# Layer 0 of a four-layer network: work moved between ScalarE and VectorE, the first keys broadcast in two parts, and a finer order at the layer's end

## The chip, the cores and the metric

The kernel runs on one core of a Trainium2 chip. Its time is that of the device, in microseconds (us), from start to end of one execution; of several runs the median is given. The core has a matrix engine (TensorE, PE in the profile; its weight loads are PEld), a vector engine (VectorE, DVE), an engine for functions of one argument (ScalarE, ACT), a general one (GpSimd, POOL) and a queue engine for transfers (SyncE, SP). Each runs its own instructions in order and waits on semaphores for the others. Matrix products go to PSUM[...]; the rest lies in SBUF.

## The reference, cut to what matters

Four layers follow one another; the change concerns layer 0, a deformable attention with a multilayer perceptron behind it. For 2 images of 512 channels and 32 x 32 pixels, in 8 groups of 64 channels:

```python
xn = _bn(x, bn1_g, bn1_b)
q = _gconv1x1(xn, qw)
off = conv(q, off_dw_w, stride 4, 6 x 6 taps, each channel alone)
off = gelu(off + off_dw_b)
off = tanh(einsum(off, off_pw_w)) * 4.0
vgrid = 2.0 * (key's own place + off) / 7 - 1.0
kv = _grid_sample(xn, vgrid)            # bilinear, 64 keys a group
k, v = _gconv1x1(kv, kw), _gconv1x1(kv, vw)
pos = grid_q[:, :, None, :] - grid_kv[:, None, :, :]
bias = sign(pos) * log1p(abs(pos))
bias = relu(bias @ cpb_w1 + cpb_b1)
bias = relu(bias @ cpb_w2 + cpb_b2)
bias = bias @ cpb_w3 + cpb_b3
attn = softmax(q k / 8 + bias)
x = x + out_w (attn v) + out_b
x = x + mlp(_bn(x))
```

The bias costs most: for each of 16 pairs of image and group, 1024 queries times 64 keys go through two layers of 128 hidden units. All of it is in fp32.

## The kernel before, in words

**Tiles and loops.** Two groups lie on the 128 partitions at a time; the eight such pairs of groups are what the code calls pairs. A bias unit `u` is one group of one image (16 of them), and it has 8 octets `o` of 8 keys, each cut into two halves `jj` (the kernel's index for keys 0 to 31 and 32 to 63). One step of the main loop, a quad, is one (u, o, jj): four keys for all 1024 queries. There are 256 quads. For each, `first_hidden` (L475 on) lets VectorE make four tiles `h` of 128 x 1024 as a sum of a table along x and one along y (L484); `second_hidden` (L495 on) multiplies them by the second layer's weights, 64 matmuls in four column groups (L515), into four accumulators `hp`, which ScalarE evicts (L520). ScalarE and GpSimd then flip signs and GpSimd adds them up, partly with accumulating DMAs (L507). `last_product` (L547) multiplies by ones at the ends.

**Tables.** `table` (L430 on) gives each pair of octets its logs: a DMA broadcasts 16 keys' logs from DRAM to all partitions, GpSimd makes the x table (L440), and VectorE the y table for each octet (L472). The y table lies in a PSUM bank called `bank`, which also holds the taps of the convolution, the results of small products, and the x weights `wp` of the sampling. The first 16 keys of all don't go through DRAM: 32 matmuls (L449) with a column of the identity spread the logs of pair 0 to all partitions, and ScalarE evicts them (L457, L461).

**Work that goes along.** `offsets` (L279 on) and `sampled` (L361 on) are generators: the first makes a pair's queries, the convolution of 36 taps (L311: six products; L325: three reductions), Gelu, tanh, the key positions and their logs; the second the bilinear weights `w` (L377 to L397), the sampled values (L404), keys and values. Pair 0's `offsets` runs alone ahead of the main loop. The others advance by one step per quad, behind the matmuls of that quad; `attend` has the first right to such a step. `odd` holds a generator back until a quad with `jj` = 1, whose successor needs no new y table in `bank`.

**The order.** Inside layer 0, PE, ScalarE, VectorE and GpSimd run in the order in which the code is written (`manual_schedule`); a planner places what lies outside of it, such as the MLP's sums on VectorE (L672 to L675), between those instructions. PSUM has three buffers of two banks for everything in the pool `ps_h` (`hp`, the transposes, `q`), one bank for `bank`, and one for the similarities `sim`. Two engines that touch one bank of one tile are put in order with a wait.

**The end.** The last unit's attention (`attend`, L555 on) runs alone: its softmax goes back and forth between PE, VectorE and ScalarE. `share` (L193 on) lays the output projection's matmuls (L200) between those steps, for three of four output tiles; the fourth follows in `project_one` (L647), and the MLP begins.

Of the kernel before, what the change touches and what calls it, by code (L numbers as in the profile page):

```python
# [11 lines left out]
F32 = mybir.dt.float32  # L12
# [6 lines left out]
P = 128  # L19
# [23 lines left out]

G_KEY, G_QRY, G_X, G_Y = 0, 2, 2 + W, 2 + W + 1
NGRID = G_Y + NB
# [7 lines left out]
class Net:  # L53
# [43 lines left out]
    def layer0(self):  # L97
# [3 lines left out]
        with ExitStack() as ctx:  # L101
# [7 lines left out]
            self.last_weights(keep)  # L109
# [25 lines left out]
            with self.tc.manual_schedule(engines=engines):  # L135
                pairs = [{} for _ in range(BP)]
                for n, _ in enumerate(self.offsets(pairs[0], 0, ps)):
                    if n == 7:
                        nc.vector.tensor_copy(self.ys, self.grid[:, G_Y : G_Y + NB])
                        self.fold_weights()  # L140
# [42 lines left out]
                next(share)  # L183
                self.last_product(*held[1], sims, ps_s)
                for n, _ in enumerate(self.attend(u, pairs[u // 2], sims.pop(u), att, None)):
                    if n in (0, 1):
                        next(share)
                for _ in share:
                    pass
                for h in range(2):  # L190
                    self.project_one(ps, att, ow, "out_b", B - 1, CT - 1, h)

    def share(self, accs, att, w):  # L193


        nc = self.nc
        for t in range(CT):
            for o, acc in enumerate(accs):
                for h in range(2):
                    nc.tensor.matmul(  # L200
                        acc[:, h, :],
                        lhsT=w[:, t, o * P : (o + 1) * P],
                        rhs=att[t][:, h * HF : (h + 1) * HF],
                        start=(t == 0),
                        stop=(t == CT - 1),
                    )
                if t == CT - 1:
                    xt = self.xs[B - 1][o].rearrange("p (h x) -> p h x", h=2)
                    nc.vector.scalar_tensor_tensor(xt, acc, self.col("out_b", o), xt, ALU.add, ALU.add)
            if t < CT - 1:  # L210
                yield

    def last_weights(self, keep):

        nc = self.nc
        self.w3row = keep.tile([P, P], F32, tag="row", name="w3row")
        nc.scalar.dma_start(self.w3row, self.io["cpb_w3"].partition_broadcast(P))  # L220
        w3 = self.colr("w3r", 4)
        self.magb = keep.tile([P, 4], F32, tag="magb", name="magb")
        nc.vector.scalar_tensor_tensor(self.magb, w3, -1.0, w3, ALU.mult, ALU.max)
        nc.vector.tensor_tensor(self.magb, self.magb, self.colr("b2r", 4), ALU.mult)
        sign = keep.tile([P, 4], F32, tag="sign", name="sign")
        nc.vector.tensor_scalar(sign, w3, 0.0, 2.0, ALU.is_ge, ALU.mult)
        nc.vector.tensor_scalar(sign, sign, -1.0, None, ALU.add)
        self.flip = keep.tile([P, 3], F32, tag="flip", name="flip")
        nc.vector.tensor_tensor(self.flip, sign[:, 0:3], sign[:, 3:4].to_broadcast([P, 3]), ALU.mult)
        self.ends = keep.tile([P, 60], F32, tag="ends", name="ends")  # L230
        nc.vector.memset(self.ends, 0.0)
        for k in range(4):
            rows = slice(32 * k, 32 * k + 32)
            nc.vector.tensor_copy(self.ends[rows, 28 + k : 29 + k], sign[rows, 3:4])
# [44 lines left out]
    def offsets(self, m, bt, ps):  # L279
# [11 lines left out]
        q = ps.tile([P, 2, HF], F32, tag="ps", name=f"q{b}{t}")  # L291
        for par in range(2):
            rows = slice(par * DH, (par + 1) * DH)
            for h in range(2):
                nc.tensor.matmul(
                    q[h * DH : (h + 1) * DH, par, :],
# [5 lines left out]
        for par in range(2):  # L302
            for h in range(2):
                (nc.scalar.copy if h == par else nc.vector.tensor_copy)(
                    qp[par * DH : (par + 1) * DH, 1 + 16 * h : 17 + 16 * h, 1 : 1 + W],
                    q[h * DH : (h + 1) * DH, par, :].rearrange("p (r w) -> p r w", w=W),
# [3 lines left out]
        for ky in range(6):  # L310
# [13 lines left out]
        for third in (slice(0, 24), slice(24, 44), slice(44, NJ)):  # L324
            nc.vector.tensor_reduce(conv[:, third], prod[:, :, :, third].rearrange("p a b j -> p j (a b)"), AX.X, ALU.add)  # L325
            yield
        ge = self.fpool.tile([P, NJ], F32, tag="ge", name=f"ge{b}{t}")
# [8 lines left out]
        nc.scalar.activation(at, o, AF.Tanh)  # L336
        yield
# [19 lines left out]
        nc.sync.dma_start(spots, at)  # L357
# [3 lines left out]
    def sampled(self, m, bt, ps):  # L361
# [6 lines left out]
        g = self.fone.tile([P, 2, 2 * NJ], F32, tag="g", name=f"g{b}{t}")  # L368
# [4 lines left out]
        for n in range(NB):  # L373
# [3 lines left out]
        nc.vector.tensor_scalar(g, spots.rearrange("p k d -> p d k"), 1.0, W / 2.0, ALU.add, ALU.mult)  # L377
        wx = self.fone.tile([P, 2 * NJ], F32, tag="wx", name=f"wx{b}{t}")
        nc.vector.tensor_scalar(wx, g[:, 0, :], -0.5, self.grid[:, G_X : G_X + 1], ALU.add, ALU.subtract)
        nc.vector.tensor_scalar(g[:, 1, :], g[:, 1, :], -0.5, None, ALU.add)  # L380
# [3 lines left out]
            g[:, 1, :].unsqueeze(1).to_broadcast([P, NB, 2 * NJ]),  # L384
# [4 lines left out]
        nc.scalar.activation(wx, wx, AF.Abs)  # L389
        nc.scalar.activation(w, w, AF.Abs)  # L390
        yield
        nc.vector.tensor_scalar(w, w, -1.0, 1.0, ALU.mult, ALU.add)
        yield
        wp = self.bank[:, 384:512]
        nc.vector.tensor_scalar(wx, wx, -1.0, 1.0, ALU.mult, ALU.add)
        nc.vector.tensor_scalar(wp, wx, 0.0, None, ALU.max)
        nc.vector.scalar_tensor_tensor(w, w, 0.0, wp.unsqueeze(1).to_broadcast([P, NB, 2 * NJ]), ALU.max, ALU.mult)  # L397
# [32 lines left out]
    def table(self, u, o, pairs, tables):  # L430
# [12 lines left out]
        if u == o == 0:  # L443

            logs = self.ps_h.tile([P, 2, 8, 2, W], F32, tag="ps", name="lb_ps")
            for j in range(2):
                for k in range(8):
                    key = j * 32 + k
                    nc.tensor.matmul(  # L449
                        logs[:, j, k, :, :].rearrange("p d x -> p (d x)"),  # L450
                        lhsT=self.ident[:, key : key + 1].to_broadcast([P, P]),
                        rhs=pairs[0]["log"].rearrange("p d x -> p (d x)"),
                        start=True,
                        stop=True,
                    )
            x = self.tab.tile([P, 2, 8, W], F32, tag="x", name="tx00")
            nc.scalar.activation(  # L457
                x, logs[:, :, :, 0, :], AF.Identity, scale=self.col("cpb_w1", 0), bias=self.col("cpb_b1")
            )
            got = self.lpool.tile([P, 2, 8, 2, W], F32, tag="logs", name="lb00")  # L460
            nc.scalar.copy(got, logs)  # L461
            tables["logs"], tables["x"], tables["rest"] = logs, x, got
        elif o % 2 == 0:
# [4 lines left out]
        if u == 0 and o == 1:  # L468
            tables["logs"] = tables.pop("rest")
        y = self.bank[:, 0:256].rearrange("p (j i x) -> p j i x", j=2, i=4)  # L470
        i = 4 * (o % 2)
# [169 lines left out]
    def project_one(self, ps, att, w, bias: str, b: int, o: int, h: int):  # L641
# [3 lines left out]
        acc = ps.tile([P, HF], F32, tag="ps", name=f"{bias}_{b}{o}{h}")  # L645
# [993 lines left out]
def _grid():  # L1639
# [6 lines left out]
    rows[:, G_X] = p % W  # L1646
    for n in range(NB):
        rows[:, G_Y + n] = n * (P // W) + p // W
    return rows
# [73 lines left out]
```

## Time and profile before

| | |
|---|---|
| median of 3 runs | 3410.36 us (3410.17 to 3419.77) |
| profiled execution | 3411.19 us, of it 3409.2 us span |
| PE busy | 3354.4 us, 98% |
| VectorE, ScalarE, GpSimd busy | 2417.5, 2026.5, 2172.1 us |
| first matmul of the main loop (L515) | 35.62 us after the start |
| last matmul of layer 0 ends, MLP begins | 2069.91 and 2070.80 us after the start |
| L515, hidden products | 16384 matmuls (an fp32 product counts twice) |
| L484, first hidden layer | 1024 on VectorE, 1.215 us each |
| L520, evictions | 1024 on ScalarE, 1.112 us each |

The span is the time between the first and the last instruction of one execution. Busy time counts overlapping instructions once; an instruction's place is given by its line (L515 is line 515 of the kernel). Matmuls are pipelined: four that work in different column groups run at the same time, so whether PE is at its pace is read from the distance between their starts.

### The profile page before, as it was taken

To read this page: it belongs to the slowest core of one execution; us is meant where nothing else is said; L and a number is where in the kernel's file an instruction comes from. 1 tells how busy PE (TensorE), PEld (TensorE's weight loads), DVE (VectorE), ACT (ScalarE), POOL (GpSimd) and SP (SyncE) were. 2 spreads that over 40 slices of the span, in tenths; PEclk is the share of its full clock that TensorE was granted. 3 is DMA by queue.
4 is the path that set the end of the run, shared out by engine and by line. 5 is a ranking of instruction groups with operands and counts; after the bars stand their busy time and mean duration, and the time that the engine had idled before them with its cause. 6 is when DMAs were issued, how large, how long until landed. Compare 5 with 4: busy or idle time off the path is not lost.

```text
span 3409.2 us, 60195 instructions
## 1 busy us (share of the span) xinstructions
PE 3354.4 (98%) x25248; PEld 1246.9 (37%) x25248; DVE 2417.5 (71%) x2591; ACT 2026.5 (59%) x2109; POOL 2172.1 (64%) x1642
## 2 busy tenths in 40 slices
PE   6999999999999999999999999999999999999999
PEld 2333333333333333333333334444555433355433
DVE  6876877777776676777776665565465689765897
ACT  5787877877877687877877771111121466213662
POOL 3777878877877577877878874333333448444474
PEclk9999999999999999999999999999999999999999
DMA  5878877877877577877878862111000100000001
GB/s 150 158 150 157 160 147 153 164 147 150 167 145 147 118 152 155 164 148 149 167 157 167 160 134 107 37 50 37 0 1 0 38 1 1 14 0 13 1 1 51
DMA packets 102382, 342.63 MB, mean 101 GB/s; under 512 B 12624, under 2 KB 14288, under 8 KB 99024
## 3 DMA queue, kind: packets, MB, share of 16 engines
q0 software_dynamic: 73296, 266.90, 41.2%
q1 hardware_dynamic: 27792, 69.68, 7.1%
q8 instruction: 202, 3.31, 0.4%
q10 hardware_dynamic: 1008, 2.06, 0.2%
q14 instruction: 84, 0.69, 0.1%
HBM read 67.27 MB, written 4.46 MB: 21 GB/s over the span
## 4 chain that ended last, share of the span: by engine, by line
PE 90%; DVE 6%; POOL 2%; ACT 1%; DMA 1%; issue 1%; DVEq 0%; ACTq 0%; POOLq 0%; SPq 0%
PE hp L515 50%; PE s L1323 5%; PE o L1352 5%; PE sim L547 3%; PE qk20P L1109 1%; PE qk30P L1109 1%; PE m_0P L686 1%; PE m_6P L686 1%; PE m_3P L686 1%; PE m_2P L686 1%; PE m_1P L686 1%; PE qk31P L1109 1%; PE qk21P L1109 1%; PE m_5P L686 1%; PE m_4P L686 1%; PE m_7P L686 1%
## 5 line engine op out<-in xcount | busy, mean ns | idle before, releaser
L515 PE MATMUL hp<-h,w 128*32 128x512 f32 x16384 | 1822.4, 593 | 5.3 <-DVE h L484 3.6
L484 DVE CUSTOM_DVE_ANT_1 h<-tx,bank 128x1024 f32<-128x1024 f32 x1024 | 1180.0, 1215 | 277.1 <-PE hp L515 241.6
L520 ACT ACTIVATE h<-hp,magb 128x1024 f32<-128x1024 f32 x1024 | 1121.8, 1112 | 405.1 <-PE hp L515 398.4
L515 PEld LDWEIGHTS hp<-h,w 128*32 128x32 f32 x16384 | 530.5, 110 | 1221.7 <-issue 1154.6
L507 POOL DMA_DIRECT2D h<-h x509 | 451.8, 1021 | 411.3 <-ACT h L526 350.5
L533 POOL TENSOR_TENSOR h<-h,h 128x1024 f32<-128x1024 f32 x255 | 610.3, 2393 | 21.3
L531 POOL TENSOR_SCALAR h<-h,flip 128x1024 f32<-128x1024 f32 x256 | 446.6, 1745 | 0.9 <-ACT h L520 0.9
L1327 ACT ACTIVATE e<-s 128x1024 f32<-128x1024 f32 x256 | 261.9, 1025 | 159.6 <-PE s L1323 158.3
L522 ACT ACTIVATE h<-h,flip 128x1024 f32<-128x1024 f32 x256 | 291.4, 1138 | 0.0
L1352 PE MATMUL o<-e,v 64*64 64x512 f32 x2048 | 267.7, 589 | 0.8 <-ACT e L1327 0.8
L1323 PE MATMUL s<-q,k 64*64 64x512 f32 x2048 | 267.9, 589 | 0.0
L1332 POOL TENSOR_TENSOR some<-e,e 128x1024 f32<-128x1024 f32 x32 | 75.6, 2364 | 171.7 <-DVE sum L1341 138.7
L1334 POOL TENSOR_TENSOR some<-some,e 128x1024 f32<-128x1024 f32 x64 | 166.8, 2607 | 24.9 <-ACT e L1327 21.2
L524 POOL TENSOR_SCALAR h<-h,flip 128x1024 f32<-128x1024 f32 x128 | 144.5, 1129 | 47.7 <-ACT h L520 46.6
L526 ACT ACTIVATE h<-h,flip 128x1024 f32<-128x1024 f32 x128 | 145.6, 1138 | 0.0
L547 PE MATMUL sim<-h,ends 128*32 128x512 f32 x1024 | 142.4, 592 | 0.0
L1352 PEld LDWEIGHTS o<-e,v 64*64 64x64 f32 x2048 | 83.4, 133 | 137.4 <-issue 132.2
L1323 PEld LDWEIGHTS s<-q,k 64*64 64x64 f32 x2048 | 83.2, 133 | 136.0 <-issue 123.7
L664 POOL TENSOR_TENSOR mlp_w<-mlp_w 128x512 f32<-128x512 f32 x16 | 22.4, 1402 | 160.8 <-DMA mlp_w<-in_mlp_w 136.3
L1337 DVE TENSOR_TENSOR sum<-e,e 128x1024 f32<-128x1024 f32 x32 | 79.5, 2484 | 64.0 <-ACT e L1327 63.9
L745 ACT ACTIVATE mh<-mh,cols 128x512 f32<-128x512 f32 x64 | 46.1, 722 | 124.3 <-DVE mh L763 65.5
L1375 DVE RECIPROCAL r<-r 128x512 f32<-128x512 f32 x32 | 107.3, 3353 | 1.1
(530 smaller groups left out, 3343.9 us busy)
## 6 DMA issues: line engine op xcount, KB each, us to landing
h<-h POOLq DMA_DIRECT2D x509, 512.0 KB, 6.5
lb<-logs SPq DMA_DIRECT2D x63, 512.0 KB, 5.2
mlp_w<-in_mlp_w SPq DMA_DIRECT2D x16, 1024.0 KB, 4.9
x<-in_x SPq DMA_DIRECT2D x8, 512.0 KB, 9.5
qkw<-in_l_qk SPq DMA_DIRECT2D x2, 2048.0 KB, 8.1
out<-x SPq DMA_DIRECT2D x16, 256.0 KB, 2.7
vw<-in_l_v SPq DMA_DIRECT2D x2, 1024.0 KB, 7.9
projw<-in_l_proj SPq DMA_DIRECT2D x2, 1024.0 KB, 4.8
```

The lines of the kernel that those rows point to most:

```text
L484: self.nc.vector._custom_dve(TENSOR_ADD_SAT, out=h[:, k, :, :], in0=x[:, jj, 2 * r + k, :].unsqueeze(1).to_broadcast([P, H, W]), in1=y[:, ...
L507: nc.gpsimd.dma_start(to, what, accum_op=ALU.add)
L515: nc.tensor.matmul(hp[rows, cut], lhsT=self.l0w2[:, 32 * q : 32 * q + 32], rhs=h1[k][:, cut], start=True, stop=True)
L520: nc.scalar.activation(y, hp, AF.Relu, bias=self.magb[:, q : q + 1])
L522: nc.scalar.activation(ys[0], ys[0], AF.Copy, scale=self.flip[:, 0:1])
L531: nc.gpsimd.tensor_scalar(y, y, self.flip[:, 2:3], 1.0, ALU.mult, ALU.mult)
L533: (nc.vector if final else nc.gpsimd).tensor_tensor(y, y, ys[2], ALU.add)
L547: nc.tensor.matmul(sims[u][at : at + 32, :], lhsT=self.ends[:, 28 - 4 * o : 60 - 4 * o], rhs=z[jj][:, h * HF : (h + 1) * HF], start=(o == ...
L686: self.nc.tensor.matmul(acc[p], lhsT=w[:, a, k, p * P : (p + 1) * P], rhs=right(r, k), start=k == 0, stop=k == 1)
L1323: nc.tensor.matmul(s[halves[c], par, :], lhsT=ks[p][rows, at : at + DH], rhs=qs[p][rows, cut], start=True, stop=True)
L1327: nc.scalar.activation(e, s, AF.Exp, scale=DH**-0.5)
L1352: nc.tensor.matmul(o[halves[par], r, :], lhsT=v[n // 2][rows, n % 2, at : at + DH], rhs=e[rows, par, :], start=(n == 0), stop=(n == NB - 1),)
```

## The change

It consists of seven edits, all in layer 0.

- **Pair 0's queries** get two PSUM tiles instead of one. VectorE evicts both halves of the one, ScalarE both of the other.
- **Pair 0's convolution**: the products of the last three rows of taps are made by ScalarE, in 18 instructions of 64 elements with the tap as a scale; VectorE makes the first three rows. The reduction is done in two halves and a sum.
- **The signs and magnitudes of the last layer's weights** (`last_weights`) are worked out behind pair 0's Gelu instead of at the very start. Only their DMA stays there. A tiny logarithm behind pair 0's tanh calls for the table of Ln.
- **The first keys** are spread in two parts of eight, one for o = 0 and one for o = 1. VectorE multiplies the logs by a mask cut from the identity, and one matmul with a matrix of ones for each of the two coordinates sums over the partitions. The second part, and its two matmuls, come one octet later.
- **Sampling weights**, for all eight pairs: the positions are scaled by ScalarE before they go to DRAM; of the weights VectorE keeps one subtraction and one product, and ScalarE takes the absolute values with their offsets and the two clamps (Relu of 1 - w), among them the one that writes `wp` into `bank`. An `odd` step stands ahead of the clamps.
- **The end**: `share` yields after each output tile (two matmuls) instead of after three, and the steps are laid anew: three before the last products, one behind the scores, three behind the maximum, one before and one after the product with the values.
- **The last output tile** is accumulated in `bank` and in `sim`'s bank instead of in `ps_h`.

```diff
@@ layer0
-            self.last_weights(keep)
+            self.all = keep.tile([P, P], F32, tag="all", name="all")
+            nc.gpsimd.memset(self.all, 1.0)
+            last_weights = self.last_weights(keep)
+            next(last_weights)
...
-                    if n == 7:
+                    if n == 4:
                         nc.vector.tensor_copy(self.ys, self.grid[:, G_Y : G_Y + NB])
+                        next(last_weights, None)
                         self.fold_weights()
...
-                next(share)
+                for _ in range(CT - 1):
+                    next(share)
                 self.last_product(*held[1], sims, ps_s)
-                for n, _ in enumerate(self.attend(u, pairs[u // 2], sims.pop(u), att, None)):
-                    if n in (0, 1):
+                sim = sims.pop(u)
+                for n, _ in enumerate(self.attend(u, pairs[u // 2], sim, att, None)):
+                    for _ in range({0: 1, 1: 3, 4: 1, 5: 1}.get(n, 0)):
                         next(share)
                 for _ in share:
                     pass
-                for h in range(2):
-                    self.project_one(ps, att, ow, "out_b", B - 1, CT - 1, h)
+                for h, acc in enumerate((self.bank, sim)):
+                    self.project_one(acc, att, ow, "out_b", B - 1, CT - 1, h)
@@ offsets
+        qs = [q[:, par, :] for par in range(2)]
+        if bt == 0:
+            qs[1] = ps.tile([P, HF], F32, tag="ps", name="q001")
...
-                (nc.scalar.copy if h == par else nc.vector.tensor_copy)(
+                (nc.scalar.copy if (par if bt == 0 else h == par) else nc.vector.tensor_copy)(
...
+        own = 3 if bt == 0 else 6
+        for ky in range(own, 6):
+            for kx in range(6):
+                nc.scalar.activation(
+                    prod[:, ky, kx, :].rearrange("p (y x) -> p y x", y=8),
...
+                    AF.Copy,
+                    scale=self.col("dw_w", 6 * ky + kx),
+                )
-        for ky in range(6):
+        for ky in range(own):
...
+        if bt == 0:
+            more = self.fpool.tile([P, NJ], F32, tag="ge", name="conv_more")
+            for to, rows in ((conv, slice(0, 3)), (more, slice(3, 6))):
+                nc.vector.tensor_reduce(to, prod[:, rows].rearrange("p a b j -> p j (a b)"), AX.X, ALU.add)
+            nc.vector.tensor_tensor(conv, conv, more, ALU.add)
             yield
...
+        if bt == 0:
+            early = self.fpool.tile([P, 1], F32, tag="early", name="early_ln")
+            nc.scalar.activation(early, self.cols[:, 0:1], AF.Ln, scale=0.0, bias=1.0)
...
-        nc.sync.dma_start(spots, at)
+        g = self.fpool.tile([P, 2], F32, tag="g", name=f"g{b}{t}")
+        nc.scalar.activation(g, at, AF.Identity, scale=W / 2.0, bias=self.grid[:, G_MID : G_MID + 1])
+        nc.sync.dma_start(spots, g)
@@ sampled
-        nc.vector.tensor_scalar(g, spots.rearrange("p k d -> p d k"), 1.0, W / 2.0, ALU.add, ALU.mult)
         wx = self.fone.tile([P, 2 * NJ], F32, tag="wx", name=f"wx{b}{t}")
-        nc.vector.tensor_scalar(wx, g[:, 0, :], -0.5, self.grid[:, G_X : G_X + 1], ALU.add, ALU.subtract)
-        nc.vector.tensor_scalar(g[:, 1, :], g[:, 1, :], -0.5, None, ALU.add)
         w = self.fone.tile([P, NB, 2 * NJ], F32, tag="w", name=f"w{b}{t}")
         nc.vector.tensor_tensor(
             w,
-            g[:, 1, :].unsqueeze(1).to_broadcast([P, NB, 2 * NJ]),
+            spots[:, :, 1].unsqueeze(1).to_broadcast([P, NB, 2 * NJ]),
...
-        nc.scalar.activation(wx, wx, AF.Abs)
+        nc.scalar.activation(wx, spots[:, :, 0], AF.Abs, bias=self.grid[:, G_X : G_X + 1])
         nc.scalar.activation(w, w, AF.Abs)
         yield
-        nc.vector.tensor_scalar(w, w, -1.0, 1.0, ALU.mult, ALU.add)
-        yield
+        yield from self.odd()
         wp = self.bank[:, 384:512]
-        nc.vector.tensor_scalar(wx, wx, -1.0, 1.0, ALU.mult, ALU.add)
-        nc.vector.tensor_scalar(wp, wx, 0.0, None, ALU.max)
-        nc.vector.scalar_tensor_tensor(w, w, 0.0, wp.unsqueeze(1).to_broadcast([P, NB, 2 * NJ]), ALU.max, ALU.mult)
+        nc.scalar.activation(wp, wx, AF.Relu, scale=-1.0, bias=1.0)
+        nc.scalar.activation(w, w, AF.Relu, scale=-1.0, bias=1.0)
+        yield
+        nc.vector.tensor_tensor(w, w, wp.unsqueeze(1).to_broadcast([P, NB, 2 * NJ]), ALU.mult)
         yield
@@ table
-            logs = self.ps_h.tile([P, 2, 8, 2, W], F32, tag="ps", name="lb_ps")
-            for j in range(2):
-                for k in range(8):
...
+        if u == 0 and o < 2:
...
+            mask = self.ident.rearrange("p (j k) -> p j k", k=32)[:, 0:2, i : i + 4]
+            parts = []
+            for d in range(2):
+                at = self.fone.tile([P, 2, 4, W], F32, tag=f"first{d}", name=f"first{o}{d}")
+                nc.vector.tensor_tensor(
+                    at,
+                    pairs[0]["log"][:, d, :].unsqueeze(1).unsqueeze(2).to_broadcast([P, 2, 4, W]),
+                    mask.unsqueeze(3).to_broadcast([P, 2, 4, W]),
+                    ALU.mult,
+                )
+                got = self.ps_h.tile([P, 2, 4, W], F32, tag="ps", name=f"lb_ps{o}{d}")
+                nc.tensor.matmul(
+                    got.rearrange("p j k x -> p (j k x)"),
+                    lhsT=self.all,
...
+                parts.append(got)
+            x = tables["x"][:, :, i : i + 4, :]
+            nc.scalar.activation(x, parts[0], AF.Identity, scale=self.col("cpb_w1", 0), bias=self.col("cpb_b1"))
+            nc.vector.tensor_scalar(y, parts[1], self.col("cpb_w1", 1), None, ALU.mult)
+            return x, y
```

The constants that the kernel is given change with it: the column for x holds its negative, and one column holds 15.5, the middle of the 32 pixels.

## The prediction

> **What bounds the kernel now.** I read the stages first (the busy time of each engine in stretches of the span; after the length come PE, PEld, DVE, ACT and POOL).
>
> ```profile
> 0.00:36.00 36.00, 9.80 (x45) 7.68 (x46) 15.63 (x34) 7.88 (x12) 0.99 (x10) 1.00 0.56 193
> 36.00:48.00 12.00, 12.00 (x72) 4.75 (x70) 9.59 (x10) 5.34 (x6) 0.73 (x1) 1.00 0.15 43
> 48.00:2036.00 1988.00, 1986.23 (x18190) 609.49 (x18188) 1456.04 (x1460) 1573.72 (x1552) 1551.89 (x1247) 1.00 0.78 153
> 2036.00:2071.00 35.00, 32.34 (x101) 13.58 (x98) 24.66 (x30) 2.08 (x4) 23.37 (x17) 1.00 0.33 127
> ```
>
> The change touches layer 0 alone, which ends at 2071 us. Three things can be won there: PE's 26 idle us of the first 36, what hides in the loop's 1988, and 2.7 of idle PE at the end. The chain of waits, in order of time, tells what fills the start:
>
> ```profile
> 12.23 4.54 DVE prod L311 x6
> ...
> 22.91 1.28 ACT L350
> ...
> 25.01 7.07 PE lb_ps L449 x32
> ...
> 35.62 11.55 PE hp L515 x64
> ```
>
> The first pair's offsets are one serial chain; PE copies 16 keys' logs to all partitions with 32 small matmuls before any hidden unit can be made.
>
> The loop looks full, but busy PE is not PE at its pace. A quad is 64 matmuls in four column groups, four at a time. The timeline of PE, one common quad and one at 469 us:
>
> ```profile
> 406.40 7.07 PE L515 MATMUL hp<-h,w 128*32 128x512 f32 x64
> ```
> ```profile
> 468.99 9.92 PE L515 MATMUL hp<-h,w 128*32 128x512 f32 x63
> ```
>
> Taking the starts of the matmuls sixteen at a time, a group takes 1.71 us; those beginning at 468.99, 716.58, 964.06, 1484.51 and 1732.06 take 2.49 longer, though no idle PE is shown: the four groups of columns run one after the other, each waiting for its part of h. VectorE's timeline just before says why:
>
> ```profile
> 461.47 0.69 DVE L595 COPY pt<-pp 128x512 f32<-128x512 f32 x1 [3.70 <-PE pp L591]
> 462.08 1.10 DVE L377 TENSOR_SCALAR g<-at 128x256 f32<-128x256 f32 x1
> 463.22 2.37 DVE L379 TENSOR_SCALAR wx<-g,grid 128x128 f32<-128x128 f32 x1
> 465.51 0.21 DVE L380 TENSOR_SCALAR g<-g 128x128 f32<-128x128 f32 x1
> 465.76 1.22 DVE L382 TENSOR_TENSOR w<-g,bank 128x1024 f32<-128x1024 f32 x1
> 467.01 0.49 DVE L472 TENSOR_SCALAR bank<-lb,cols 128x256 f32<-128x256 f32 x1
> 467.63 6.87 DVE L484 CUSTOM_DVE_ANT_1 h<-tx,bank 128x1024 f32<-128x1024 f32 x6
> ```
>
> The sampling weights stand ahead of h; h starts at 467.63, and four of 1.13 end at 472.2, while PE wants the first at 468.99. The same sequence stands before the other four. At 228 and 1252 us, where no attention step shares the slot, L379 took 0.29 and 0.69, and PE loses nothing. So 5 x 2.49 = 12.4 us of the loop are VectorE's lateness.
>
> The end, again PE's timeline:
>
> ```profile
> 2054.70 0.66 PE L591 MATMUL bank<-ident,e 128*128 128x128 f32 x4 [0.16 <-DVE e L587]
> 2056.14 0.43 PE L606 MATMUL bank<-pt,v 64*64 64x256 f32 x2 [0.78 <-DVE pt L595]
> ...
> 2057.63 5.42 PE L200 MATMUL ob<-att,ow 128*128 128x512 f32 x12 [0.83 <-ACT att L619]
> ```
>
> With 0.89 before the MLP's first matmul at 2070.80 that makes 2.66 us.
>
> [...] L379's 2.37 us end when GpSimd's L533 (463.12, 2.39 us) ends. [...] the four evictions L304 stand in single file (ACT 9.49, DVE 10.11 and 10.82, ACT 11.54). [...] sets of L515 start 0.85 us apart until 41.2 us and 0.43 after, with a granted clock of 1.00.
>
> [...] the Gelu took 347. [...] L382 took 1222.
>
> **The start, step by step** (before, then after).
> - Nine small instructions on cols leave the path ahead of xn (1.0 us), but the q weights, issued at 1.17, landed 5.9 us later, at 7.07: q starts at 7.12 instead of 7.44. Gain 0.3, not 1.0.
> - Evictions: q ends at 9.10, then DVE 2 x 0.70 beside ACT 2 x 0.58 in other banks. Products start at 10.6 instead of 12.23.
> - Products: DVE 3 x 0.755 to 12.85, first half reduction (half of 4.12) to 14.9. ACT's 18 from 10.6: no row of before has this form[...]. From below 0.16 (L350 to L351, no pointer): 13.6; from above 0.35, no overlap: 16.9. I take 0.25. Second half to 17.3, addition 0.2 (L353's 0.23): Gelu at 17.5 instead of 20.94.
> - Gelu to tanh unchanged, 1.0: 18.55. The weights' small instructions now stand on DVE here: 1.2 us as at 5.34 to 6.54, beside the 0.67 at 20.83. DVE is free at 19.35, so L338 to L341 wait 0.8 and end at 19.98. Meanwhile ACT does the early table load and Ln (1.28 + 0.2) to 20.0, which hides it. Abs, Ln, Sign and the product then take 0.95: 20.95 instead of 24.87.
> - First keys: [...] the two fp32 products with ones are four passes over 256 columns, each half of L515's cold 0.85 plus some 0.1 of weights, to 23.8. Then L472 0.49 and h 1.23: first hp at 25.65 instead of 35.62, 10.0 earlier. [...]
> - The price of it: keys 4 to 7 now take two more products in PE's queue behind the transposes L374, in the same three PSUM buffers. That is 1.0 us of PE, 0.3 of wait for q3's eviction (in the profile to 48.97) and 0.4 for the copy xnT (to 49.88), which now releases the next hp. Together 1.8. DVE's y for o=1 comes later by 6 us, but h for it is due only at 56.8 in the old frame.
>
> Start: 10.0 - 1.8 = 8.2[...]. Ends: 5.5 and 10. The spots DMA leaves about when logs does on SP's queue, and lb after it; they land within 9 us, and w is wanted 20 us later: hidden. w3row's DMA keeps its place on ACT's queue, and the memset of ones joins GpSimd, whose first loop work stands at 47.27.
>
> **The loop.** DVE loses L377, L379, L380, L392, L395, L396. At 462.08 there is only w (1.22) and y (0.49): h runs from 463.9 to 468.5, before 468.99. All five losses go: 12.4. ACT gets Relu of 1024 (1.04 as L390) and of 128 (0.3), and one tiny activation for g, per pair. They come after a quad with five ACT pieces of about 1.03 in 6.87, so they fit in the 1.7 free; if the cover went, 8 x 1.3 us. New: wp is written by ACT in the bank where y lies, so h of the next quad waits for it, behind q3's eviction. The tanh of L336 is the same wait today: DVE starts h at 407.53, done at 412.1, due at 414.2; no loss. Lower end 8, upper 13.5.
>
> **The end.** Finer steps hide the waits of 0.78 and 0.83: two matmuls (1.75 us) stand in each. But after ss only two matmuls stand before the transposes: sim ended at 2043.60, ss at 2045.80, so PE waits 0.55. Maximum to normalised e takes 4.4 us, with 5.3 of PE to cover it, if VectorE is free. It isn't: L673 to L675 of the MLP (1.22 each, 2.29 once GpSimd works, from 2047.8) are placed by the planner between them. With one of them ahead and one in the exponent's gap, waits are 0.55 + 1.2 + 0.6 against 1.77: 0.5 worse. With all three ahead, 1.7 worse; with none in the way 1.2 better. I take 0.6 worse. The 0.89 stays: PE started 0.1 after the last addition L651, and the MLP's eight banks include that accumulator wherever it lies.
>
> Sum: 8.0 + 12.4 - 0.6 = 19.8. The profiled run took 3411.19 (span 3409.2 and 2 us around it): 3391.4; the median before is 0.8 lower, 3410.36: 3390.6, say 3391.
>
> **Rivals.**
> 1. The loop gains nothing: h is late for another reason, or ACT's part takes the place. [...] Then 8.0 - 0.6 gained: 3403.
> 2. Slower: the wait of h for ACT's wp. It costs from where wp comes 1.7 us later than the tanh of today. To end above 3420.6 it must eat 20 + 10 us, 3.8 in each of 8 pairs, so wp 5.5 us late; ACT, at 1574 of 1988 us, would need a backlog of a whole quad. About 3422.
> 3. The start disappoints: ACT's products at 0.35 and the reductions slower, and all three MLP additions ahead: 5 + 10 - 1.7, so 3397.
>
> **Numbers.** Forecast 0.70, rival 3 0.12, rival 1 0.12, rival 2 0.06. Range: all gains at the upper end (10 + 13.5 + 1) give 3386, the lower (5.5 + 8 - 1.7) 3398.6; towards rival 1 I stretch to 3400. 0.3% is 10 us, about what a measurement of this kernel tells from none: faster 0.82, same 0.12, slower 0.06.
>
> **What would show it.** First L515 near 25.7; Gelu near 17.5; PE waits of some 0.7 in all ahead of the second quad; no group of sixteen 2.49 long; L377 and L379 gone and h started before its quad; gaps before the transposes and pp at the end. Wrong if h still waits, on ACT's wp, or if new long groups appear where ACT has the Relus.

## The result, and the profile after

The changed kernel takes 3387.23 us (median of 4 runs, 3386.91 to 3387.65) against 3411.25 for the kernel before on the same chip (4 runs): ratio 0.9926, 95% interval 0.9912 to 0.9940. It is 24.0 us faster where 19.8 were forecast, and lies inside the range of 3386 to 3400. The profiled execution took 3386.91, with a span of 3385.1, 24.1 less than before.

The experiments' medians carry a few microseconds of another kind, since the granted clock differs between executions (means of 0.996 to 1.000) and with it the time behind layer 0 (1339.2 us in the changed kernel's profile at 0.999, 1344.9 in e2's and 1347.2 in e3's, both at 0.997). So small effects are read below from four points of the trace: the first hidden matmul, the second quad's first matmul, the first output product (the loop's end) and the MLP's first matmul. Two profiles of the changed kernel agree in them within 0.4 us. The kernel before, measured again beside every group of experiments, took 3411.3 to 3411.8 us.

| | before | after | shorter by |
|---|---|---|---|
| first hidden matmul at | 35.62 | 26.82 | 8.80 |
| second quad at (start) | 48.12 | 40.09 | 8.03 |
| second quad to first output product (loop) | 1988.21 | 1972.72 | 15.49 |
| first output product to the MLP (end) | 34.47 | 33.15 | 1.32 |
| from there on | 1338.4 | 1339.2 | -0.8 |

The stages of the changed kernel, with the same columns as the stages shown of before (length; busy PE, PEld, DVE, ACT, POOL; clock; DMA share; GB/s):

```profile
0.00:27.00 27.00, 4.59 (x17) 1.98 (x18) 14.57 (x33) 12.62 (x31) 1.19 (x11) 1.00 0.64 233
27.00:40.00 13.00, 12.58 (x76) 5.07 (x74) 8.34 (x10) 7.18 (x8) 2.47 (x3) 1.00 0.42 107
40.00:2012.00 1972.00, 1971.03 (x18185) 609.39 (x18188) 1417.04 (x1414) 1582.52 (x1575) 1548.26 (x1245) 1.00 0.77 154
2012.00:2046.00 34.00, 32.52 (x103) 13.30 (x97) 22.18 (x30) 1.38 (x4) 21.89 (x17) 1.00 0.33 128
```

In the loop VectorE has 39 us less to do and ScalarE 9 more, yet the stage is 16 shorter, and neither engine fills it: the amount of work doesn't explain the 16.

**The start.** In the changed kernel's timelines, this is ScalarE's part of the tap products, then VectorE's second reduction, then PE from the products with ones to the second quad:

```profile
10.57 5.48 ACT L326 ACTIVATE prod<-qpad,cols 128x64 f32<-128x64 f32 x18 [0.34 <-DVE qpad L317]
```
```profile
16.08 2.08 DVE L352 TENSOR_REDUCE conv_more<-prod 128x64 f32<-128x1152 f32 x1 [1.10 <-ACT prod L326]
```
```profile
22.73 2.05 PE L499 MATMUL lb_ps<-first,all 128*128 128x256 f32 x4 [3.50 <-DVE first L492]
26.82 10.52 PE L559 MATMUL hp<-h,w 128*32 128x512 f32 x64 [2.04 <-DVE h L528]
37.27 1.09 PE L413 MATMUL tr<-ident,xn 128*128 128x128 f32 x8
...
39.19 0.70 PE L499 MATMUL lb_ps<-first,all 128*128 128x256 f32 x2 [0.31 <-ACT h L564]
40.09 2.35 PE L559 MATMUL hp<-h,w 128*32 128x512 f32 x20 [0.20 <-ACT xnT L414]
```

The 18 products took 5.48 us, their starts 0.30 apart, and the second reduction waited 1.10 us for them. The two short waits ahead of the second quad are those of the forecast. From the transposes tr to the second quad PE takes 2.82 us (37.27 to 40.09), and 1.02 in the kernel before (to 48.12):

```profile
47.10 1.09 PE L374 MATMUL tr<-ident,xn 128*128 128x128 f32 x8
```

The 8.80 us of the first hidden matmul are made up so: q starts 0.45 earlier, and then these stretches are shorter: q and its evictions, up to the first tap product (by 1.25), from there to the Gelu (0.8), from the Gelu to the end of log (0.25), and from log to the first hidden matmul (6.05).

**The loop.** VectorE's timeline at the slot that stood at 462 us before, then PE's:

```profile
454.05 1.21 DVE L418 TENSOR_TENSOR w<-at,bank 128x1024 f32<-128x1024 f32 x1
455.30 0.49 DVE L516 TENSOR_SCALAR bank<-lb,cols 128x256 f32<-128x256 f32 x1
455.92 9.15 DVE L528 CUSTOM_DVE_ANT_1 h<-tx,bank 128x1024 f32<-128x1024 f32 x8
```
```profile
460.93 7.07 PE L559 MATMUL hp<-h,w 128*32 128x512 f32 x64
467.82 1.04 PE L591 MATMUL sim<-h,ends 128*32 128x512 f32 x8
...
490.25 1.15 PE L440 MATMUL bank<-w,xnT 128*64 128x64 f32 x32
```

The quad at 460.93 now takes 7.07, not 9.92. And the gain is larger than that quad's. PE's timeline of the kernel before, from the same late quad on:

```profile
468.99 9.92 PE L515 MATMUL hp<-h,w 128*32 128x512 f32 x63
478.33 0.60 PE L547 MATMUL sim<-h,ends 128*32 128x512 f32 x3
478.75 0.59 PE L515 MATMUL hp<-h,w 128*32 128x512 f32 x1
478.76 1.01 PE L547 MATMUL sim<-h,ends 128*32 128x512 f32 x4
...
501.60 1.15 PE L404 MATMUL bank<-w,xnT 128*64 128x64 f32 x32
```

The sum products sim, eight in one piece after, are here cut up between hidden products: the four groups of columns are out of step. h comes in four tiles, one for each group, and the first matmuls of the four groups start at 468.99, 470.04, 471.16 and 472.29. By then the first three groups have done two matmuls each, and all four go on together. So the fourth is two matmuls (2 x 0.43 us) behind the others, and it stays so for three more quads. The groups fall into step at L404, whose matmuls use more than one of them. From the late quad's start to there it is 32.61 us before (468.99 to 501.60) and 29.32 after: 3.29 for one slot, as much as the fourth group starts behind the first (3.30). Of it 2.49 show in the first group of sixteen, and 0.8 where the groups meet again. Lining up the two traces eviction by eviction shows the same step, 3.26, at each of the five slots and none above 0.2 that lasts elsewhere.

**The end.** PE's timeline of the changed kernel; the first line is the last sum products but one:

```profile
2010.65 2.22 PE L591 MATMUL sim<-h,ends 128*32 128x512 f32 x8
2012.81 5.42 PE L208 MATMUL ob<-att,ow 128*128 128x512 f32 x12
...
2021.83 0.60 PE L618 MATMUL bank<-ident,ss 128*128 128x128 f32 x4
...
2028.17 0.65 PE L635 MATMUL bank<-ident,e 128*128 128x128 f32 x4 [0.59 <-DVE e L631]
...
2045.96 1.52 PE L729 MATMUL m_0P<-mx,mlp_w 128*128 128x512 f32 x3 [0.89 <-POOL mlp_w L709]
```

No wait is left ahead of the first transposes and 0.59 ahead of the second; the 0.89 before the MLP stayed. Two of the MLP's additions still stand on VectorE inside the softmax, one ahead of the maximum (2023.28) and one between it and the subtraction (2025.01):

```profile
2022.15 1.22 DVE L717 TENSOR_TENSOR mx<-mx,mx 128x1024 f32<-128x1024 f32 x1
...
2023.88 1.22 DVE L718 TENSOR_TENSOR mx<-mx,mx 128x1024 f32<-128x1024 f32 x1
```

But the last sums of the loop took 2.22 us where they took 1.04 before: they wait 1.0 for a DMA of h, and this stage's gain hangs on that (below).

### The profile page after: what moved, and what is told of

Its sections match the earlier page's. It is cut to its first block, busy times and chain, and to the rows that moved or that the text cites. A ratio compares the mean times of both kernels' runs of the same rounds, so it can differ in the third digit from the quotient of the medians.

```text
span 3385.1 us, 60157 instructions
## 1 busy us (share of the span) xinstructions
PE 3335.1 (99%) x25224; PEld 1241.3 (37%) x25224; DVE 2377.3 (70%) x2544; ACT 2040.8 (60%) x2152; POOL 2169.6 (64%) x1643
## 4 chain that ended last, share of the span: by engine, by line
PE 90%; DVE 6%; POOL 2%; ACT 1%; issue 1%; DMA 0%; ACTq 0%; DVEq 0%; POOLq 0%
PE hp L559 51%; PE s L1366 4%; PE o L1395 4%; PE sim L591 3%; PE qk20P L1152 1%; PE qk30P L1152 1%; PE m_0P L729 1%; PE m_6P L729 1%; PE m_4P L729 1%; PE m_2P L729 1%; PE m_1P L729 1%; PE qk31P L1152 1%; PE qk21P L1152 1%; PE m_5P L729 1%; PE m_3P L729 1%; PE m_7P L729 1%
## 5 line engine op out<-in xcount | busy, mean ns | idle before, releaser
L559 PE MATMUL hp<-h,w 128*32 128x512 f32 x16384 | 1799.3, 593 | 3.0 <-DVE h L528 2.0
L528 DVE CUSTOM_DVE_ANT_1 h<-tx,bank 128x1024 f32<-128x1024 f32 x1024 | 1180.8, 1216 | 308.6 <-PE hp L559 236.8
L577 POOL TENSOR_TENSOR h<-h,h 128x1024 f32<-128x1024 f32 x255 | 610.0, 2392 | 21.3
L591 PE MATMUL sim<-h,ends 128*32 128x512 f32 x1024 | 135.3, 592 | 0.1
```

The source lines that it names most:

```text
L528: self.nc.vector._custom_dve(TENSOR_ADD_SAT, out=h[:, k, :, :], in0=x[:, jj, 2 * r + k, :].unsqueeze(1).to_broadcast([P, H, W]), in1=y[:, ...
L559: nc.tensor.matmul(hp[rows, cut], lhsT=self.l0w2[:, 32 * q : 32 * q + 32], rhs=h1[k][:, cut], start=True, stop=True)
L577: (nc.vector if final else nc.gpsimd).tensor_tensor(y, y, ys[2], ALU.add)
L591: nc.tensor.matmul(sims[u][at : at + 32, :], lhsT=self.ends[:, 28 - 4 * o : 60 - 4 * o], rhs=z[jj][:, h * HF : (h + 1) * HF], start=(o == ...
```

## The experiments

In e1 to e4 one part of the change is undone. The evictions of q and the small instructions moved behind the Gelu have no run of their own, so what they are worth is read from the two timelines alone.

**e1, the sampling weights on VectorE again.**

```diff
+        nc.vector.tensor_scalar(g, spots.rearrange("p k d -> p d k"), 1.0, W / 2.0, ALU.add, ALU.mult)
+        nc.vector.tensor_scalar(wx, g[:, 0, :], -0.5, self.grid[:, G_X : G_X + 1], ALU.add, ALU.subtract)
+        nc.vector.tensor_scalar(g[:, 1, :], g[:, 1, :], -0.5, None, ALU.add)
...
-        nc.scalar.activation(wp, wx, AF.Relu, scale=-1.0, bias=1.0)
-        nc.scalar.activation(w, w, AF.Relu, scale=-1.0, bias=1.0)
```

> The changed kernel with one part undone: the sampling weights are made on VectorE again, as in the kernel before. Theory A (VectorE's lateness ahead of h in single slots is the loop's gain): the groups of sixteen matmuls that take 2.49 us longer come back, five of them, perhaps with the two smaller losses of the kernel before (0.86 and 1.67); the run is 12.4 to 15.5 us slower than the changed kernel's 3387.2, 3400 to 3403, and start and end stay as they are. Rival B (the loop gained by the shift of the start against the loads, or by the steps' new order, not by the work taken off VectorE): at most 3 us slower, no long groups.

3403.84 us (3401.99 to 3406.23). The loop is 1989.59, 16.9 longer than after; start (second quad at 40.41) and end (33.08) stay. Lined up with the changed kernel it falls back by 3.26 at each of the five slots. Theory A holds, above the upper end of its numbers.

**e10, the kernel before with this part alone.** The reverse edit, on the kernel before.

> The kernel before with the sampling weights on ScalarE and nothing else of the change. Theory A: the five slots gain 3.3 us each wherever the start lies, 16.5 in all; the MLP's first matmul comes at about 2054.3 instead of 2070.80, and the run at 3394 to 3395. By the prediction's 2.49 a slot it would be 12.4, 3399. Rival B (it is the shift of the start against the loads that lets h be in time): under 5 us gained.

3397.06 us (3395.07 to 3400.26); the MLP's first matmul at 2052.42, 18.4 earlier than before. The loop is 1971.48, 16.7 shorter, with the same 3.26 a slot. So the gain doesn't need the new start. Of the remaining 1.7, 0.4 lie in the end (34.10 against 34.47; the MLP's addition L675 took 1.22 there and 2.29 before) and 1.3 at the start: the first hidden matmul is 0.2 earlier, and the first quad, up to the transposes, takes 10.38 us and not 11.48 for the same 64 matmuls. Before's 11.48 is the longest of fourteen profiles: the other thirteen have 10.3 to 11.1, the changed kernel 10.45. The sets of matmuls start more than 0.43 us apart for 5.8 us in it and for 3.8 to 5.0 in the others, and 0.43 apart from there on. So about 1 us of the start's 8.03 most likely belongs to that one execution and not to the change.

**e5 and e6, is it GpSimd's work or the number of instructions?** What the expectations call a lock is this: in the kernel before L379 took 2.37 us and ended with GpSimd's L533 (at 463.22), and it took 0.29 at 228.20, where GpSimd had been done since 228.02. Here there is one more instruction behind w for each of the pairs 1 to 7, on data that nobody reads, and then the same with its output in PSUM.

```diff
+        if bt:
+            nc.vector.tensor_scalar(self.spare, self.ident, -0.5, 1.0, ALU.add, ALU.subtract)
```
```diff
+        if bt:
+            nc.vector.tensor_scalar(self.bank[:, 384:512], self.ident, -0.5, 1.0, ALU.add, ALU.subtract)
```

> The changed kernel with one more VectorE instruction for each of the pairs 1 to 7: a TENSOR_SCALAR of 128x128, SBUF to SBUF, on data that nobody reads, just behind w, where the weights of the kernel before stood. Theory A (the lock by GpSimd made the weights long, and what is long there delays h): in the slots of the pairs 2, 3, 4, 6 and 7 it takes about 2.2 us instead of 0.2 to 0.3, h ends 1.7 us after PE wants its first part, and each slot costs PE 1 to 2.6 us: the MLP's first matmul is 5 to 13 us later than the changed kernel's 2045.96. Rival B (the number of VectorE's instructions counts, not the lock): 0.3 us longer, 0 to 1.5 us in all.

> The same as the run with the extra SBUF instruction, the same operation, size, source and place, but with its output in a PSUM bank. Theory A, by the trace (L516 of the changed kernel, a TENSOR_SCALAR from SBUF to PSUM, takes its 0.49 beside GpSimd's work): not locked, 0.3 us each; h still ends before PE wants it, and the MLP's first matmul stays within 0.5 us of 2045.96. If it is locked too, it costs the same 5 to 13 us, and the pair doesn't separate lock and count.

e5: 3397.31 us (3397.25 to 3397.60), and the MLP 9.1 later. e6: 3387.27 (3387.20 to 3388.68), the changed kernel's own time, and the MLP 0.2 later. VectorE's timelines in the same slot, e5 first:

```profile
455.39 2.37 DVE L426 TENSOR_SCALAR spare<-ident 128x128 f32<-128x128 f32 x1
457.68 0.47 DVE L519 TENSOR_SCALAR bank<-lb,cols 128x256 f32<-128x256 f32 x1
458.29 9.14 DVE L531 CUSTOM_DVE_ANT_1 h<-tx,bank 128x1024 f32<-128x1024 f32 x8
```
```profile
455.63 0.29 DVE L425 TENSOR_SCALAR bank<-ident 128x128 f32<-128x128 f32 x1
455.96 0.49 DVE L518 TENSOR_SCALAR bank<-lb,cols 128x256 f32<-128x256 f32 x1
456.57 9.14 DVE L530 CUSTOM_DVE_ANT_1 h<-tx,bank 128x1024 f32<-128x1024 f32 x8
```

The place of the output alone makes 2.37 us of 0.29 (median of the seven in e5 2.373, all seven in e6 0.295). In e5 GpSimd's L580 runs from 455.30 to 457.68 there, and the instruction ends 0.1 us behind it; at 221.14, where GpSimd is idle, the same instruction took 0.22. In e6 GpSimd is at work in the same way (L579, from 455.43 to 457.82), and the instruction is done in 0.29. Why the place of the output counts, no trace here shows.

In e5 h starts 2.2 us later than in the changed kernel (458.29 against 455.92, less 0.2 by which the whole start is later), and each of the five slots loses 1.74; in the kernel before h was 3.68 late in that frame (467.63 less 8.03, against 455.92) and the slot lost 3.26. So by these two points a slot has some 0.4 us of slack, and behind it each microsecond of lateness of h is a microsecond of PE.

**e7, wp in SBUF.** The wait of h for ScalarE's wp, which rival 2 rested on, is taken away.

```diff
-        wp = self.bank[:, 384:512]
+        wp = self.fone.tile([P, 2 * NJ], F32, tag="wp", name=f"wp{b}{t}")
```

> The changed kernel with wp in SBUF and not in the PSUM bank where y lies. Of the prediction's rival 2 (h waits for ScalarE's wp): in the changed kernel VectorE's h waits 34.8 us in 8 times for wp. Theory A: that wait is inside slack, so taking it away moves the MLP's first matmul by less than 0.5 us either way, unless the product of w and wp, now with both sources in SBUF, is locked by GpSimd and comes late. If the wait costs, the run gets faster, up to 8 x 0.8.

3387.38 us; the loop 1972.66 against 1972.72. The 34.8 us of waits were slack: they are gone, and in their place h waits 26 us more for PE (263.0 against 236.8). The product of w and wp, whose sources now both lie in SBUF, takes 1.26 to 2.21 us (L433), and 1.21 in the changed kernel, and PE loses nothing by that either.

**e3, the first keys by 32 small matmuls again.** The function for the tables is that of the kernel before.

> The changed kernel with the first keys undone: 16 keys' logs are copied to all partitions by 32 small matmuls again. From the end of log to the first hidden matmul it was 10.7 us before and is 4.9 now, and the second quad no longer has products in its way (some 1 us): theory A expects the first hidden matmul 5.8 us later, the second quad 5 us later and the run 5 us slower, 3392. Rival C (a shorter start is eaten by the wait of later steps for their loads): under 2 us slower.

3395.16 us (3392.02 to 3400.84); the profiled execution has 1347.2 us from the MLP on, against 1339.2. By the trace's points the first hidden matmul is 6.4 later (33.21; q started 0.25 later), the second quad 4.4 and the MLP 4.9. Theory A holds. Its loop and end say more: 1971.55 and 34.80, where after has 1972.72 and 33.15. PE's timeline of the end in e3:

```profile
2015.10 1.04 PE L583 MATMUL sim<-h,ends 128*32 128x512 f32 x8
...
2025.60 0.66 PE L610 MATMUL bank<-ident,ss 128*128 128x128 f32 x4 [0.34 <-DVE ss L606]
...
2033.09 0.66 PE L627 MATMUL bank<-ident,e 128*128 128x128 f32 x4 [1.68 <-DVE e L623]
```

Here sim waits for no DMA, and the finer steps have the waits that the prediction named, 0.34 and 1.68: 0.3 us worse than the 34.47 before, and 0.7 worse than e10's 34.10. In the changed kernel PE is held up 1.2 us by the DMA at the loop's end, and VectorE goes on with the MLP's instructions in that time: the last six instructions that make mx start 1.80 us ahead of the second sum products sim (2016.35 against 2018.15), and 0.62 ahead in e3 and in the kernel before. So they are further out of the way of the softmax, and the end's gain is bought with the loop's loss. The transfers in the 10 us behind the issue of the last two (by queue: packets, MB, share of 16 engines; by issue: KB each, median us to landing), the changed kernel first, then e3:

```profile
q0 software_dynamic: 288, 1.05, 54.0%
q8 instruction: 1, 0.02, 0.6%
h<-h POOLq DMA_DIRECT2D x2, 512.0 KB, 7.0
```
```profile
q0 software_dynamic: 288, 1.05, 53.5%
h<-h POOLq DMA_DIRECT2D x2, 512.0 KB, 5.4
```

A packet of an instruction queue falls among the last two transfers of h, which then land 7.0 us after issue and not 5.4. It takes 0.98 us (from 2006.61); each transfer ends with sixteen packets of 4 bytes, and of the last transfer's fifteen are through at 2009.85 and the sixteenth at 2011.45, while in e3 all sixteen are through within 0.15 us. All eleven profiles of kernels with products by ones have that packet there and the longer landing (6.7 to 7.1); the three of kernels with 32 small matmuls (before, e3, e10) have no such packet, and 5.4 to 5.6. No run moves the packet alone, and why it comes there was not tried.

**e2, the end's steps and accumulators as before.**

```diff
-                for _ in range(CT - 1):
-                    next(share)
+                next(share)
                 self.last_product(*held[1], sims, ps_s)
...
-                for h, acc in enumerate((self.bank, sim)):
+                for h in range(2):
+                    acc = ps.tile([P, HF], F32, tag="ps", name=f"last{h}")
```

> The changed kernel with the end undone: coarse steps of the output products, and the last accumulators from the three rotating PSUM buffers. The prediction had the finer steps cost 0.6 us, so undoing them would make it 0.6 us faster; the changed kernel's trace has the stretch from the first output product to the MLP's first matmul 1.3 us shorter than before, so by that undoing costs 1.3 us: 3388.5. The waits of 0.78 and 0.83 ahead of the last sample's products come back.

3393.20 us (3389.38 to 3394.16); in the profiled execution 5.7 us lie after the MLP's start (1344.86 against 1339.17), where nothing was edited. Its end is 34.10 against 33.15, with 0.78 and 0.83 back. So beside the late DMA the finer steps gain 0.95. Without it they don't: the old end takes 34.10 too in e10, where the DMA comes in time, and the finer steps 34.80 in e3. So, set against e10, neither the late DMA nor the finer steps shorten the end alone, and together they do.

**e4, no sharing of the tap products.**

```diff
-        own = 3 if bt == 0 else 6
+        own = 6
```

The reductions are over all taps again, in three parts, and the step behind which `last_weights` goes on is counted anew, so that it stays behind the Gelu.

> The changed kernel with all 36 tap products of the first pair on VectorE, and the three reductions over all taps; evictions by half and the rest stay. The prediction's terms make the sharing worth 1.8 us (8.7 from first product to Gelu, against 6.9). The changed kernel's trace has 7.9, since ScalarE's products came 0.30 us apart and the second reduction waited 1.10 us for them: by that it is 0.8 us slower than the changed kernel, 3388.0, and the first hidden matmul is 0.8 us later than 26.82.

3390.08 us; the first hidden matmul at 27.89, 0.9 to 1.0 later than in e1 and e2 (26.92 and 26.97), the second quad at 41.10 against their 40.41 and 40.28. Since q started 0.1 to 0.2 later here, the sharing is worth 0.8, as the trace said, not the 1.8 of the forecast's terms.

**e8, two repairs at the start.**

```diff
-            nc.scalar.dma_start(self.l0qkv[:, 0], io["l0_qkv"][:, 0])
+            nc.scalar.dma_start(self.l0qkv[:, 0, 0], io["l0_qkv"][:, 0, 0])
...
+            nc.scalar.dma_start(self.l0qkv[:, 0, 1:CT], io["l0_qkv"][:, 0, 1:CT])
...
-        own = 3 if bt == 0 else 6
+        own = 4 if bt == 0 else 6
```

> The changed kernel with two edits at the start: the q weights of the first pair alone are loaded first (64 KB instead of 256, the rest behind the other small loads), and VectorE makes four rows of tap products, ScalarE two. q now waits for its weights until 6.99, and xn is there at 5.93; ScalarE's 18 products ended 1.10 us after the first reduction. Expected: q at 6.0 to 6.5, Gelu 0.4 to 0.5 earlier by the rows, the first hidden matmul at 25.4 to 26.0 instead of 26.82, and the run 0.8 to 1.4 us faster than the changed kernel. If the load is as late as before (its latency and not its size), only 0.4.

3386.93 us. q at 6.76 (7.14 to 7.22 in the three other runs beside it): a quarter of the bytes lands 0.4 us earlier, so most of the wait is not size. q and the first hidden matmul (26.11) stay just outside what was expected. The second quad is at 39.49 and the MLP at 2045.24: 0.7 earlier than in the changed kernel and 1.1 earlier than in e7 beside it. The time itself is 0.3 shorter, which is too little to tell.

**e9 and e11, the long instruction that is left.** In the changed kernel pos of pair 1 takes 2.29 us at 176.79, beside GpSimd's L577 (from 176.62 to 179.00), where the median of the eight is 0.225. Both build on e8. e9 puts pos in the PSUM bank; e11 drops it, with the distance as the bias of ScalarE's Abs and Sign.

```diff
-        pos = self.fpool.tile([P, 2, W], F32, tag="pos", name=f"pos{b}{t}")
+        pos = self.bank[:, 256:320].rearrange("p (d x) -> p d x", d=2)
```
```diff
-        nc.scalar.activation(log, pos, AF.Abs)
+        for d in range(2):
+            nc.scalar.activation(log[:, d, :], qry, AF.Abs, bias=at[:, d : d + 1])
```

> The run with the two start edits, and pos (the distances of a pair's keys to the queries) in PSUM instead of SBUF. In the changed kernel pos of pair 1 is the one of eight that GpSimd locks: 2.29 us instead of 0.23, at 176.8; h behind it starts at 179.61 and the quads at 183.84 and 195.29 lose 0.31, 0.4 and 1.69. Theory A: with pos in PSUM it takes 0.3, h is in time, and that quad's loss and its skew go, 1.2 to 2.0 us; the run ends near 3385.3 against 3386.9 with the start edits alone. Rival: the loss there comes from ScalarE's two table loads at 193.16 and 195.24, and nothing changes; or a product of two SBUF sources is locked wherever its output goes, and pos stays at 2.3.

> The run with the two start edits, and VectorE's pos gone: ScalarE takes the distance as the bias of its Abs and of its Sign, two small instructions each in place of one (the offsets' second step is negated for it). The run with pos in PSUM left pos locked at 2.29 us, and made y wait 6.83 us for ScalarE's write in the bank. Theory A: without pos nothing of pair 1 is locked, h there starts about 2 us earlier, the quad at 182.6 and its skew lose nothing: 1.3 to 2.0 us less in the loop than the run with the start edits, whose loop is 1972.3; start 0 to 0.4 earlier; near 3385. Rival: ScalarE's two table loads hold the loop up there in any case, and nothing is gained.

> The changed kernel again, unaltered, on the same chip as the run without pos, to compare the two: 3387.2, as before, within 1 us; first hidden matmul within 0.3 of 26.8, second quad within 0.4 of 40.1, the MLP's first matmul within 0.5 of 2046.

e9: 3391.30 us, its loop 1974.89, 2.6 longer than e8's 1972.29. VectorE's timeline of e9:

```profile
176.81 2.29 DVE L379 TENSOR_TENSOR bank<-grid,at 128x64 f32<-128x64 f32 x1
...
197.05 0.49 DVE L517 TENSOR_SCALAR bank<-lb,cols 128x256 f32<-128x256 f32 x1 [6.83 <-ACT bank L389]
```

With two sources in SBUF it still takes 2.29 us, though its output is in PSUM, as the second rival had it (it ends 0.1 us behind GpSimd's L578, which runs from 176.64 to 179.01), and y now waits 6.83 for ScalarE's late write in its bank; PE falls 2.4 us behind e8 right there. That is the wait of the prediction's rival 2 at another place. e11: 3386.72 us (3386.49 to 3390.21) beside 3388.20 (3387.24 to 3394.69) for the changed kernel again, no difference that can be told. Its timelines of VectorE and then of PE at that place:

```profile
176.81 4.61 DVE L526 CUSTOM_DVE_ANT_1 h<-tx,bank 128x1024 f32<-128x1024 f32 x4
```
```profile
182.12 7.07 PE L557 MATMUL hp<-h,w 128*32 128x512 f32 x64
...
196.44 4.07 PE L557 MATMUL hp<-h,w 128*32 128x512 f32 x36 [1.24 <-ACT h L562]
```

VectorE has no pos there, h starts 2.8 us earlier (0.5 of it by the start), the quad is whole, and lined up with the changed kernel e11 gains 1.64 us there. Then 0.56 goes back at ScalarE's two table loads, where PE waits 1.24, and 0.1 to 0.2 at each of five later pairs, 1.0 in all: the loop is 1972.61 against 1972.54. So theory A has the slot right and the sum wrong. The later losses stand where ScalarE has two more instructions; that these are the cause is argued only. Of all kernels run none is measurably faster than the changed one.

## Why the prediction was right, and where not

- **q at 7.12, products at 10.6.** They started at 6.99 and 10.53.
- **ScalarE's products 0.25 apart, Gelu at 17.5.** The term, the author's estimate between the bounds of 0.16 and 0.35, was too small: they are 0.30 apart (397 ns each). This is the step that failed in the start. They end at 16.05 and not at the 15.2 that starts 0.25 apart would give, the reduction waits 1.10 us, and the Gelu is at 18.45. Rival 3's cause was real, at half its size.
- **VectorE free at 19.35, log done at 20.95.** The moved small instructions do stand on the path, and they took 2.2 us (18.42 to 20.61) and not the 1.85 of the forecast. log is done at 22.13: 0.95 late by the Gelu and 0.2 by these.
- **Keys in 4.7 us, first hidden matmul at 25.65.** The 4.7 was right (22.13 to 26.82; the two masked products in it, the author's estimate, took 0.42 each, L492), so all of the 1.2 by which the first hidden matmul is late comes from the two terms above: it is 8.8 earlier, not 10.0.
- **The price of 1.8 at the second quad.** It was right: 2.82 less 1.02. But the first quad took 10.45 us in place of before's 11.48, most likely by chance of that execution (e10). So the 8.0 of the start was met by luck: two errors of one microsecond cancel.
- **The loop's 12.4.** Cause, place and number of slots hold (e1, e10, e5, e6); the size of one is 3.3 and not 2.49. The failed step is "those ... take 2.49 us longer": only the group of sixteen that ran late was counted, and not the 0.8 that the columns' skew costs at the next matmul that needs them together. Five slots are 16.3 and smaller places give 0.4; the late DMA at the loop's end takes 1.2 back.
- **The end's 0.6 worse.** It became 1.3 better in the changed kernel, and 0.3 worse in e3, where the DMA comes in time and VectorE stands to PE as the forecast assumed. The failed step is that the MLP's instructions stand relative to PE as before: they stand 1.2 us earlier. The result has the size of the case "none in the way" (1.2 better), but that is not what happened: two of the three additions still stand in the softmax, and PE's output products cover all of it but 0.59.
- **Rivals.** 1, the loop gains nothing: fell with e1 and e10. 2, wp eats the gain: fell with e7. 3 came true in part, in ScalarE's products.

The sum: the span is 24.1 shorter, 19.8 were forecast. The loop gave 3.1 more, the end 1.9 more, the start nothing more or less, and 0.8 was lost behind layer 0, where the change touches nothing. The loop's 15.5 and the end's 1.3 both lie above their own upper ends, 13.5 and 1; the time stayed inside the range, near its fast end, because the start gave 8 of its upper 10 and 0.8 was lost behind layer 0.

## What to carry to other kernels

When PE runs in groups of columns, lateness of one group's input shows neither as idle time nor in full in the late piece (here 2.49 of 3.29 us): line up the starts, before and after, up to the next instruction that needs all columns, and look for instruction groups that are cut into each other. Look up the VectorE instructions beside a busy GpSimd one by one: here one more for each of seven pairs made the MLP 9.1 us later with its output in SBUF (median 2.37 us each) and 0.2 later with it in PSUM (0.29), so where the operands lie counted more than how many instructions there were; moving the output of an instruction with two SBUF sources left it at 2.29. And undo each part alone: here two errors of the start cancelled, and the end's gain came only with a delay at the loop's end, which the sum alone would not have shown.

## What was not expected of the hardware

- A late part of h costs a slot 3.29 us, of which 0.8 falls some 30 us later, when the groups of columns meet: for three quads the fourth group ran two matmuls behind the others.
- The same TENSOR_SCALAR took 2.37 us beside GpSimd's work with its output in SBUF (e5) and 0.29 with it in PSUM (e6); a TENSOR_TENSOR with two SBUF sources took 2.29 with its output in PSUM too (e9).
- One 0.02 MB packet of an instruction queue stood among two transfers of 0.5 MB each, which then landed in 6.7 to 7.1 us and not in 5.4 to 5.6: eleven profiles with it, three without.
- 64 elements with stride and a pointer for a scale took ScalarE 397 ns (L326 of the changed kernel), the starts 299 apart in a row.
